# The loop over groups of a graph layer kernel, issued in source order instead of a scheduler's order

## The chip, the cores and the metric

The kernel runs on one core of a Trainium2 chip. The metric is the device time of one execution in microseconds. The core has four engines that compute: TensorE (PE in the profile; its weight loads are listed apart as PEld), VectorE (DVE), ScalarE (ACT) and GpSimd (POOL). SyncE (SP) issues the DMAs. TensorE writes its results to PSUM, from where VectorE and ScalarE read them.

## The reference, cut to what matters

There are 128 graphs of 128 nodes with 64 features. Layer 0 sums, for each node j, a ReLU over the neighbours that the mask of the adjacency matrix names. Layer 1 is a message pass with a gated update. Both end in a residual and a layer norm.

```python
# layer 0, per graph b
mask = (adj > 0.0)
h  = relu(x @ W1a [:, :, None] + (x_j - x_k) @ W1b + b1)     # for all pairs j, k
hm = einsum('bjkh,bjk->bjh', h, mask)                        # 192 wide
x  = layernorm(x + hm @ W2 + deg * b2)
# layer 1, per graph b
m   = relu(relu(x @ W1 + b1) @ W2 + b2)
msg = relu(adj @ m)
r, z, n = gates(msg @ W_ih.T + b_ih, x @ W_hh.T + b_hh)
x   = layernorm(x + (1 - z) * n + z * x)
```

The first layer is rewritten as u_j + v_k for each pair with an edge, so a ReLU sum becomes a sum of absolute values over the neighbours. The neighbours of each node are put into slots by 0/1 selection matrices.

## The kernel before, in words

The 128 graphs ("samples") are handled in 32 groups of G = 4. A group's work has three parts.

**Preparation** (`prep_steps`, 18 steps): masks (L303, POOL), ranks (L308 on PE, L310 on DVE), degrees, counts (eight small POOL operations, L321 to L336), offsets, turned, rows (L360, L369 on DVE), owners, places (L382 to L391), the selection matrices `pick0` and `pick1` (L398, 21 DVE operations), and `values(i)` for each sample. A `values` step is a chain: PE multiplies into `pu` (L409), ACT writes the first bf16 piece `b0` (L410) and `u` (L411), DVE takes the rest `r` (L413), ACT writes the second piece `b1` (L414), POOL writes the third (L415).

**Slots**: 16 stretches per group. Stretch (i, k) belongs to sample i and part k = 0 to 3; it is written "step 23" for i = 2, k = 3. In each, ACT first fills three PSUM banks (`pv`) with u, which is called the seed (L440). PE then adds 18 matrix products (9 where k is 2; L468). DVE then reduces the three banks by absolute value (L474). There are two such `pv` buffers, so the seed of a stretch has to wait until the reduce of the stretch two before has read the buffer. After k = 0, `before` runs (PE L448, ACT L450 and L452, DVE L453); after k = 2 POOL adds parts (L482, L483); after k = 1 `sums` of the sample before run (PE L494 to L497, ACT L498).

**Tail** (`tail_steps`, 11 steps): the second matrix product (L189) and residual (L191), a layer norm (DVE statistics L166 and L168, then four POOL operations L170 to L175), a transpose (L202), three message steps (L207 to L221), two gate steps (L230 to L236), the update (ACT L242, POOL L244 to L250), and the second layer norm with the store.

The main loop over groups writes these parts in one mixed order. While the slots of group g are written, the tail of group g-1 and the preparation of group g+1 are written between them as "side" steps, two after each stretch. In the source, the seed of the next stretch stands before the slots of the present one, and the side steps stand after them:

```python
ahead = seed(next stretch)
slots(s, i, k, p)
if k == 1 and pend:
    sums(*pend)
...
side[n]()
```

For a group in the middle of the run the loop's arithmetic puts the side steps thus:

| step | side steps | step | side steps |
|---|---|---|---|
| 00 | none | 20 | message3, turned |
| 01 | load, masks | 21 | gates (first half), values(2) |
| 02 | residual0, ranks | 22 | gates (second half), rows |
| 03 | second (L189), values(0) | 23 | update, places |
| 10 | norm0, degrees | 30 | norm1, picks (5) |
| 11 | turn (L202), counts | 31 | owners, picks (5) |
| 12 | message1, values(1) | 32 | values(3), picks (5) |
| 13 | message2, offsets | 33 | pick1 (3 + 3) |

The kernel is written in a tile framework. [...] Each engine runs its queue in the order in which it stands. [...] Tiles with the tag `w` (the small PSUM results of all side steps) share two buffers, so a PE operation of a side step waits until the `w` tile two before it has been read.

## Time and profile before

| what | value |
|---|---|
| median of 10 runs | 1481.21 us (1478.55 to 1488.22) |
| the profiled execution's own time | 1478.4 us |
| its span | 1476.6 us, clock granted 0.982 |
| PE busy | 1292.0 us, 87% |
| PEld busy | 1142.3 us, 77% |
| DVE busy | 1042.7 us, 71% |
| ACT busy | 916.2 us, 62% |
| POOL busy | 755.7 us, 51% |
| DMA | 23.36 MB, mean 16 GB/s |

The profile shows one execution, and the busy times sum the instructions of each engine. The rank product `pc` (L308) runs once for each group: its first run is at 13.4 us, its second at 31.2 us and its last at 1361.9 us. The busy shares in 40 slices are alike from the third slice to the next to last, so the run is one long regular stretch with a short start and end.

### The profile page before, as it was taken

How to read it: one execution, taken by the hardware profiler on the slowest of the kernel's cores; microseconds unless marked ns; L12 is line 12 of the kernel's file. 1: busy time of each engine (PE TensorE's matmuls, PEld its weight loads, DVE VectorE, ACT ScalarE, POOL GpSimd, SP SyncE). 2: the span in 40 equal slices, each digit the busy share in tenths (PEclk: the TensorE clock that was granted, in tenths of full speed). 3: DMA queues.
4: the chain of work that ended last, by engine and by line, in shares of the span. 5: the costliest groups of instructions: out<-in, count | busy, mean ns of one | idle time of the engine just before them, and what ended most of it. 6: DMA issues, size and time to landing. Idle time of an engine off the chain costs nothing.

```text
span 1476.6 us, 32123 instructions
## 1 busy us (share of the span) xinstructions
PE 1292.0 (87%) x12810; PEld 1142.3 (77%) x12810; DVE 1042.7 (71%) x2265; ACT 916.2 (62%) x1666; POOL 755.7 (51%) x1134
## 2 busy tenths in 40 slices
PE   5889888989889889889899889898889898888894
PEld 3878778778778778778788778787778787777783
DVE  5877777777777777776777776777776777776761
ACT  4666666666666666666666666666666666656651
POOL 4454564554554455554555554455554555554532
PEclk9999999999999999999999999999999999999995
DMA  2000000000000000000000000000000000000000
GB/s 58 8 12 19 19 12 16 19 12 19 19 12 15 20 12 19 19 12 16 19 12 20 18 14 16 19 12 19 13 18 16 19 12 19 10 10 12 5 2 9
DMA packets 17604, 23.36 MB, mean 16 GB/s; under 512 B 2855, under 2 KB 11306, under 8 KB 17450
## 3 DMA queue, kind: packets, MB, share of 16 engines
q1 hardware_dynamic: 17450, 21.27, 4.9%
q8 instruction: 102, 1.67, 0.5%
q14 instruction: 52, 0.43, 0.1%
HBM read 17.06 MB, written 4.19 MB: 14 GB/s over the span
## 4 chain that ended last, share of the span: by engine, by line
PE 46%; DVE 27%; ACT 13%; POOL 11%; issue 3%; DMA 0%; SPq 0%; ACTq 0%; DVEq 0%; POOLq 0%
PE pv L468 22%; DVE part L474 16%; ACT pv L440 10%; DVE pick L398 5%; PE pw L189 4%; POOL maskT L303 3%; PE pu L409 3%; DVE stats L166 2%; PE pm L207 2%; PE pa L220 2%; PE ph L494 2%; PE pn L213 2%; PE pg L232 2%; POOL ub L246 2%; PE ph L495 2%
## 5 line engine op out<-in xcount | busy, mean ns | idle before, releaser
L468 PE MATMUL pv<-b,pick 128*128 128x192 bf16 x8064 | 764.2, 248 | 118.2 <-ACT pv L440 115.1
L468 PEld LDWEIGHTS <-pick 128*128 128x128 bf16 x8064 | 682.8, 99 | 187.2 <-issue 165.4
L474 DVE TENSOR_REDUCE part<-pv 128x192 f32<-128x1152 f32 (+1 forms) x512 | 611.6, 1200 | 98.3 <-PE pv L468 92.8
L440 ACT COPY pv<-u 128x1152 f32<-128x1152 f32 (+1 forms) x384 | 370.0, 964 | 135.2 <-DVE part L474 135.0
L482 POOL TENSOR_TENSOR part<-part 128x384 f32<-128x384 f32 x128 | 127.6, 997 | 275.0 <-DVE part L474 275.0
L440 ACT COPY pv<-us 128x1152 f32<-128x1152 f32 x128 | 143.7, 1123 | 104.3 <-DVE part L474 104.2
L415 POOL TENSOR_TENSOR b<-r,b 128x384 bf16<-128x384 f32 x128 | 117.5, 918 | 98.3 <-ACT b L414 98.3
L413 DVE TENSOR_TENSOR r<-pu,b 128x384 f32<-128x384 f32 x128 | 70.7, 553 | 100.0 <-ACT u L411 100.0
L498 ACT COPY hmT<-ph 96x256 f32<-96x256 f32 x128 | 47.0, 368 | 133.2 <-PE ph L497 133.1
L398 DVE TENSOR_SCALAR pick<-rankT 128x512 bf16<-128x512 bf16 x480 | 126.1, 311 | 0.0
L410 ACT CAST b<-pu 128x384 bf16<-128x384 f32 x128 | 60.1, 470 | 86.5 <-PE pu L409 86.3
L409 PE MATMUL pu<-wuv,xT 65*128 65x384 f32 x256 | 110.9, 515 | 0.8 <-ACT deg L317 0.8
L303 POOL TENSOR_SCALAR maskT<-adjT 128x512 bf16<-128x512 f32 x32 | 50.2, 1569 | 111.2 <-PE ph L497 103.1
L494 PE MATMUL ph<-ident,part 128*96 128x128 f32 x512 | 102.4, 282 | 4.0 <-POOL part L483 4.0
L495 PE MATMUL ph<-ownT,part 128*96 128x128 f32 x512 | 98.4, 274 | 0.0
L235 DVE TENSOR_TENSOR rh<-rz,pg 128x128 f32<-128x128 f32 x64 | 18.4, 287 | 100.9 <-ACT rz L233 100.9
L189 PEld LDWEIGHTS pw<-w2c,hmT 96*128 96x128 f32 x512 | 63.7, 196 | 32.7 <-issue 30.7
L166 DVE BATCH_NORM_STATS2 stats<-y 128x6 f32<-128x64 f32 x256 | 38.6, 213 | 71.3 <-POOL y L250 71.2
L497 PE MATMUL ph<-maskT,b 128*96 128x128 bf16 x768 | 85.4, 220 | 0.0
L483 POOL TENSOR_TENSOR part<-part 128x192 f32<-128x192 f32 x128 | 75.9, 593 | 10.0
L414 ACT CAST b<-r 128x384 bf16<-128x384 f32 x128 | 65.5, 512 | 21.5 <-DVE r L413 21.2
L497 PEld LDWEIGHTS <-b 128*96 128x96 bf16 x768 | 73.5, 124 | 0.0
(122 smaller groups left out, 1810.3 us busy)
## 6 DMA issues: line engine op xcount, KB each, us to landing
adjT<-in_adjT_dram SPq DMA_DIRECT2D x32, 256.0 KB, 2.7
xT<-in_xT_dram SPq DMA_DIRECT2D x32, 128.0 KB, 3.4
x<-in_x_dram SPq DMA_DIRECT2D x32, 128.0 KB, 2.1
out_dram<-o SPq DMA_DIRECT2D x32, 128.0 KB, 1.7
bias<-piece SPq DMA_DIRECT2D x6, 0.5 KB, 2.2
wb<-in_w_dram SPq DMA_DIRECT2D x1, 48.0 KB, 2.2
wa<-in_w_dram SPq DMA_DIRECT2D x1, 48.0 KB
w2c<-in_w_dram SPq DMA_DIRECT2D x2, 24.0 KB, 1.8
```

The lines of the kernel that those rows point to most:

```text
L189: nc.tensor.matmul(p[:, i, :], s["hmT"][:, i, c, :], w2c[:, c, :], start=c == 0, stop=c == 1)
L303: nc.gpsimd.tensor_scalar(s["maskT"], s["adjT"], 0.0, None, ALU.is_gt)
L398: nc.vector.tensor_scalar(s[name][:, i], s[src], float(first + i), None, ALU.is_equal)
L409: nc.tensor.matmul(p, s["xT"][:, i, :], wuv, start=True, stop=True)
L415: nc.gpsimd.tensor_tensor(s["b2"][:, i, :], r, s["b1"][:, i, :], ALU.subtract)
L440: nc.scalar.copy(v, src.rearrange("p (c b h) -> p c b h", c=1, b=1).to_broadcast(list(v.shape)))
L468: nc.tensor.matmul(v[:, q[0], q[1], :], pick[:, j, i, :], s[f"b{c}"][:, i, H : 2 * H], start=False, stop=c == 2, skip_group_check=True,)
L474: nc.vector.tensor_reduce(s["part1"] if t else s["part"][:, k, :], v.rearrange("p c b h -> p h c b"), AX.XY, ALU.add, apply_absolute_value ...
L482: nc.gpsimd.tensor_tensor(f[:, 0:2], f[:, 0:2], f[:, 2:4], ALU.add)
L494: nc.tensor.matmul(p[:, c, :], part[:, 0, cs], ident, start=True, stop=False)
L495: nc.tensor.matmul(p[:, c, :], part1[:, cs], s["ownT"][:, i, :], start=False, stop=False)
L497: nc.tensor.matmul(p[:, c, :], s[f"b{b}"][:, i, vs], s["maskT"][:, i, :], start=False, stop=b == 2)
```

## The change

The loop over groups, with the first loads and the preparation of group 0 ahead of it and the last tail behind it, is put under a `with tc.manual_schedule():` block. In it every engine is given its instructions in the order of the source. No operation, tile, pool or size is changed; the rest of the diff is indentation.

```diff
-        load(states[0])
-        if ng > 1:
-            load(states[1])
-        for st in prep_steps(states[0]):
-            st()
...
+        with tc.manual_schedule():
+            load(states[0])
+            if ng > 1:
+                load(states[1])
+            for st in prep_steps(states[0]):
+                st()
...
+            for g in range(ng):
...
+                for i in range(G):
+                    for k in range(len(stretches)):
+                        p = ahead
+                        at += 1
+                        ahead = seed(states[todo[at][0]], todo[at][1], todo[at][2]) if at < len(todo) and k + 1 else None
+                        slots(s, i, k, p)
+                        if k == 1 and pend:
+                            sums(*pend)
+                            pend = None
...
+                            side[n]()
+                            n += 1
...
+            sums(*pend)
+            for st in tail_steps(states[ng - 1], work, ps_w, G, storer(ng - 1)):
+                st()
```

Built, the two kernels hold the same instructions. In a group from the middle of the run TensorE's queue is nearly the same in both. VectorE's and ScalarE's differ: the kernel before spreads the `pick` operations singly and in pairs between the reduces and has the statistics of the first layer norm directly behind L191; the changed kernel has the picks in blocks of five and six in steps 30 to 33, and those statistics behind step 10's L453. Before, ScalarE writes `b1` (L414) after the next seed in three of the four `values` steps, and `most` (L452) late; in the changed kernel the order is always `b0`, `u`, `b1`, then the next seed.

More of the change, by code (lines that the diff above doesn't have):

```diff
@@ L503, in storer @@
             return lambda o: nc.sync.dma_start(out[:, g * G : (g + 1) * G, :], o)
-        load(states[0])
-        if ng > 1:
-            load(states[1])
-        for st in prep_steps(states[0]):
-            st()
-        todo = [(g, i, k) for g in range(ng) for i in range(G) for k in range(len(stretches))]
-        ahead = seed(states[0], 0, 0)
-        pend = None
-        at = 0
-        per = G * len(stretches)
-        for g in range(ng):
-            s = states[g]
-            first, second = [], []
-            if g > 0:
-                first = tail_steps(states[g - 1], work, ps_w, G, storer(g - 1))
-            if g + 2 < ng:
-                second.append(lambda g=g: load(states[g + 2]))
-            if g + 1 < ng:
-                second += prep_steps(states[g + 1])
-            side = [second.pop(0)] if second else []
-            while first or second:
-                if len(second) * (per + 1) >= len(first) * (per + 1) and second:
-                    side.append(second.pop(0))
-                if first:
-                    side.append(first.pop(0))
-            n = 0
-            for i in range(G):
-                for k in range(len(stretches)):
-                    p = ahead
-                    at += 1
-                    ahead = seed(states[todo[at][0]], todo[at][1], todo[at][2]) if at < len(todo) and k + 1 else None
-                    slots(s, i, k, p)
-                    if k == 1 and pend:
-                        sums(*pend)
-                        pend = None
-                    if k == len(stretches) - 1:
-                        pend = (s, i, s["part"], s["part1"])
-                    if i == 0 and k == 0:
-                        continue
-                    while n < len(side) and (n + 1) * (per - 1) <= (i * len(stretches) + k) * (len(side) + 1):
-                        side[n]()
-                        n += 1
-            for st in side[n:]:
-                st()
-            if g > 0:
-                states[g - 1].clear()
@@ L552, in adj_resnorm_kernel @@
-        sums(*pend)
-        for st in tail_steps(states[ng - 1], work, ps_w, G, storer(ng - 1)):
-            st()
+        with tc.manual_schedule():
[3 more added lines that the diff above has]
+            for st in prep_steps(states[0]):
+                st()
+            todo = [(g, i, k) for g in range(ng) for i in range(G) for k in range(len(stretches))]
+            ahead = seed(states[0], 0, 0)
+            pend = None
+            at = 0
+            per = G * len(stretches)
+            for g in range(ng):
+                s = states[g]
+                first, second = [], []
+                if g > 0:
+                    first = tail_steps(states[g - 1], work, ps_w, G, storer(g - 1))
+                if g + 2 < ng:
+                    second.append(lambda g=g: load(states[g + 2]))
+                if g + 1 < ng:
+                    second += prep_steps(states[g + 1])
+                side = [second.pop(0)] if second else []
+                while first or second:
+                    if len(second) * (per + 1) >= len(first) * (per + 1) and second:
+                        side.append(second.pop(0))
+                    if first:
+                        side.append(first.pop(0))
+                n = 0
+                for i in range(G):
[6 more added lines that the diff above has]
+                            sums(*pend)
+                            pend = None
+                        if k == len(stretches) - 1:
+                            pend = (s, i, s["part"], s["part1"])
+                        if i == 0 and k == 0:
+                            continue
+                        while n < len(side) and (n + 1) * (per - 1) <= (i * len(stretches) + k) * (len(side) + 1):
+                            side[n]()
+                            n += 1
+                for st in side[n:]:
+                    st()
+                if g > 0:
+                    states[g - 1].clear()
+            sums(*pend)
+            for st in tail_steps(states[ng - 1], work, ps_w, G, storer(ng - 1)):
+                st()
```

## The prediction

> **What bounds the kernel now.** I read first the busy shares and the chain that ended last:

> ```profile
> PE 1292.0 (87%) x12810; PEld 1142.3 (77%) x12810; DVE 1042.7 (71%) x2265; ACT 916.2 (62%) x1666; POOL 755.7 (51%) x1134
> ...
> PE 46%; DVE 27%; ACT 13%; POOL 11%; issue 3%; DMA 0%; SPq 0%; ACTq 0%; DVEq 0%; POOLq 0%
> ```

> PE is the busiest, but more than half of the chain lies on other engines: PE waits for them now and then. DMA is no part of it. Next, one group from the middle (694.42 to 738.61 us, from the k = 2 slots of step 02 to those of the next group), by its busy times and by who waited:

> ```profile
> 694.42:738.61 44.19, 39.58 (x403) 35.20 (x402) 32.25 (x70) 28.51 (x52) 23.45 (x35) 1.00 0.06 16
> ```
> ```profile
> PE pv L468 <- ACT pv L440: 3.7, 4, 2.5
> PE pc L308 <- POOL maskT L303: 0.9, 1, 0.9
> ```

> Columns of the first: length, then busy time of PE, PEld, DVE, ACT, POOL. PE is busy for 39.58 us and idle for 4.6, nearly all of it waiting for a seed. The rank product `pc` comes each 44.36 us on average ((1361.9 - 31.2) / 30), so this group stands for the run. The largest wait is one of 2.51 us, here from the timeline (start, length, engine):

> ```profile
> 729.27 0.60 DVE L166 BATCH_NORM_STATS2 stats<-y 128x6 f32<-128x64 f32 x4 [2.23 <-POOL y L250]
> ...
> 729.79 0.36 DVE L168 BATCH_NORM_AGGREGATE mv<-stats 128x2 f32<-128x6 f32 x4
> ...
> 730.07 1.32 DVE L474 TENSOR_REDUCE part<-pv 128x192 f32<-128x1152 f32 x1
> ...
> 731.48 1.12 ACT L440 COPY pv<-us 128x1152 f32<-128x1152 f32 x1 [2.33 <-DVE part L474]
> ...
> 732.66 0.57 PE L468 MATMUL pv<-b,pick 128*128 128x192 bf16 x5 [2.51 <-ACT pv L440]
> ```

> The scheduler put the second norm's statistics ahead of a reduce; POOL was late with `y`; DVE held the reduce behind it, so the seed and then PE were late. That is what a badly placed instruction costs in a queue. The `values` chain is the other place to look:

> ```profile
> 700.54 0.48 ACT L410 CAST b<-pu 128x384 bf16<-128x384 f32 x1 [2.45 <-PE pu L409]
> 700.92 0.33 ACT L411 COPY u<-pu 128x192 f32<-128x192 f32 x1
> 701.48 1.12 ACT L440 COPY pv<-u 128x1152 f32<-128x1152 f32 x1 [0.24 <-DVE part L474]
> 702.54 0.51 ACT L414 CAST b<-r 128x384 bf16<-128x384 f32 x1
> 702.95 0.31 ACT L450 COPY us<-pz 128x192 f32<-128x192 f32 x1
> ```

> The seed goes ahead of `b1` (L414). In source order it goes behind.

> **Durations.** An instruction's follower on the same engine starts about 0.1 us before its record ends: ACT's 0.48 cast is followed after 0.38, its 1.12 seed after 1.06. So I use the start-to-start distance for what merely queues, and the whole record for what depends. Distances from the timeline: slots 1.48 (0.74 for k = 2; results 0.17 later), sums 1.24, `pu` 0.67, second (L189) 1.73, `pz` 0.25, `pd` 0.16, `pt` 0.44, `pm` 0.95, `pn` 0.87, `po` 0.10, `pa` 1.00, `pr` 0.24, a gate half 1.08, places 0.66, `pq` 0.22, `pc` 0.21; together 38.1 us of PE per group. ACT: b0 0.37 (record 0.47), u 0.21 (0.32), b1 0.42, us 0.21, most 0.36 (0.46), seed 1.12. DVE: reduce 1.26 (1.35), r 0.47 (0.56), L453 0.33, statistics 0.80, five picks 1.0, each `side` 0.69, own 0.45. A hand-over costs 0.03 to 0.08.

> **What is removed.** In the changed order the second norm's statistics stand in step 30 behind its reduce and L453. Tanh starts after step 30's seed, POOL's four operations take 3.3 us (row 725.96 to 729.27), and `y` is there 1.4 us before DVE comes to it. The wait of 2.51 goes. Two waits on a seed of some 0.3 to 0.6 each go or are replaced by those below.

> **What is added**, walking a middle group step by step (distance on the late chain, minus the PE work beside it):

> 1. Step 03, values(0). From the end of `pu` to the next slots but one: 0.20 + b0 0.37 + u 0.32 + 0.05 + r 0.56 + 0.03 + b1 0.42 + seed 1.12 + 0.06 = 3.13. PE has slots 1.48, pz 0.25 and pd 0.16. Wait **1.24**.
> 2. Step 11, `turn`. The first norm's statistics now stand behind L453, which needs `most`, which stands behind that late seed. From the start of step 11's slots: seed began 1.18 before; + 1.05 + 0.21 + 0.46 + 0.05 = L453 at 0.59, + 0.33, statistics 0.88, then POOL ve, rs, yc, x 2.9 (rows 699.89 to 702.78) and hand-overs 0.14: x1 at 4.84. PE has 1.48 + 1.24. `pt` waits **2.13**, and the slots queue behind it.
> 3. Step 12, values(1): 3.13 against slots 1.48, pn 0.87, po 0.10: **0.68**. (`pm` waits 0.09 for its copy.)
> 4. Step 21, values(2): 3.13 against slots 0.74 and gates 1.08: **1.31**.
> 5. Step 22, rows: DVE does rh, n, both sides and own before reduce 23, and `places` needs own: from the slots of step 23, own at 2.65 + 0.05 + the last eight products 0.44 = 3.14, against 2.14: **1.00**; the late reduce then costs the next seed **0.26**.
> 6. Step 30: reduce, L453, statistics and five picks stand before reduce 31: 1.70 + 1.26 + 0.33 + 0.80 + 1.00 + 1.35 + 0.05 + 1.12 + 0.06 = 7.67 from the slots of step 30 to those of step 33; PE has 6.34: **1.33**.
> 7. Step 32, values(3), where b0 also waits for the seed of step 33: 2.93 from there, PE has 1.61: **1.32**. Then 0.13 for the seed of 01.
> 8. maskT (L303) behind `sums`, as now: **0.9**.

> Sum 10.4 us of PE waits. By the same count (the waits named by the profile plus the 0.17 in which the last product drains, five times) the group of before has 4.6 + 0.85 = 5.45. The difference is 4.95 us per group. Over 30 periods that is 148.5 us.

> **Start and end.** In the changed order all of group 0's preparation stands before its first seed; by the same distances (at the slow early clock of rows 13.77 to 29.28) the slots of step 03 start near 37 instead of 35.06 us: +2. Groups 0 and 31 have half of the side steps; bounds 0 to +10, I take +2 for both. The last tail, 35 us of one thin chain, keeps its order: 0. DMA: SP's load of a group waits until `message3` of step 20 frees the adjacency tile and is used in step 01 of the next group, some 28 us later at 49 us a group; a 256 KB load lands in 2.7 us, so it is covered, and the store in step 30 holds nothing back.

> Sum: 1478.4 + 148.5 + 4 = **1631 us** for the profiled execution (1476.6 span plus 1.8 around it); it lies 0.2% below the median of 1481.21, which is inside the spread.

> [...] The trace has POOL's L175 at 861 ns in the first norm, where picks run beside it, and at 612 in the second, where a reduce from PSUM does. [...]

> **Rivals.**

> - *Milder* (0.14). The waits in items 2 and 6 rest on several queues in a row; if a late PE lets the others catch up there and half of both is hidden, 1.7 us of 4.95 go: 1478 + 30 x 3.2 + 4 = 1578; with all of item 2 hidden too, 1550. For it: DVE is busy for only 32 of 44 us.
> - *Harsher* (0.13). If followers wait for whole records and not for the distances, my walk gives a period of 52.1 against 44.2: 30 x 7.9 + 4, that is 1719. Against it: rows that overlap by 0.1 throughout the trace.
> - *Faster* (0.06). The mechanism is the wait of 2.51 at step 30 that goes, with 0.75 at step 13 (slots of step 12 issued by 706.57, those of 13 from 707.32); if nothing replaces them, 30 x 3.26 less: 1381. It decides when the 3.13 us of the `values` chain finds that much PE work beside it; the rows above give 1.8 to 2.5.
> - *No change* (0.03). TensorE's queue hardly differs between the two built programs, and PE is the busiest engine; the waits might only change places: 1478 within 5. Against it: PE's order is not what makes it wait. That the region might not take effect is excluded by the built order of the other queues.

> **How the numbers follow.** The forecast (0.64) holds for 3.9 to 6.2 us per group: 1597 to 1670 with its edges. A run of this kernel can tell about 0.3% from no change. Slower: 0.64 + 0.14 + 0.13 = 0.91; same 0.03; faster 0.06. The range reaches into the milder and the harsher case: 1550 to 1705.

> **What the next profile should show.** PE idle per middle group near 9 us, by waits of `pv` on ACT, of `pt` (L202) on POOL x (L175), now 13.4 us in all, near 2 us per group, and of `ps` on DVE own; the period of `pc` near 49.3 us; POOL `y` no longer named before L166; ACT's seed directly behind `b1`. If `pt` does not wait, item 2 is wrong; if the period is under 46, the cover I counted as missing was there; if ACT or POOL show longer records, contention has entered that the trace of before does not hold.

## The result, and the profile after

The changed kernel takes 1703.17 us (median of 9 runs, 1696.48 to 1710.86) against 1481.38 for the kernel before (31 runs): 1.1484 times as long, 95% interval 1.1457 to 1.1512. It is slower, as forecast, and by more: 222 us where 152 were expected. The time lies just inside the range of 1550 to 1705, at its upper end, and outside the edges of the forecast proper, 1597 to 1670.

From the page of the changed kernel: its span, the busy shares, and the chain that ended last by engine.

```profile
span 1699.4 us, 31903 instructions
...
PE 1312.4 (77%) x12810; PEld 1148.1 (68%) x12810; DVE 1114.1 (66%) x2265; ACT 922.9 (54%) x1666; POOL 789.3 (46%) x1134
...
PE 37%; DVE 24%; POOL 19%; ACT 16%; issue 3%; DMA 0%; SPq 0%; ACTq 0%; DVEq 0%; POOLq 0%
```

Every engine has as many instructions as before; PE's busy time rose by 20 us only. POOL's share of the chain rose from 11 to 19%, though POOL is the least busy engine: others now wait for it. DVE and POOL are busy for 71 and 34 us longer with the same number of instructions, so some of their records are longer.

A middle group of the changed kernel, by its busy times (period, PE, PEld, DVE, ACT, POOL, then PE's clock):

```profile
699.36:750.65 51.29, 40.17 (x401) 35.37 (x400) 34.55 (x70) 28.73 (x53) 25.01 (x36) 1.00 0.04 14
```

And who kept PE waiting in it (us in total, times, longest):

```profile
PE pv L468 <- ACT pv L440: 7.2, 7, 1.8
PE pt L202 <- POOL x L175: 1.7, 1, 1.7
PE pc L308 <- POOL maskT L303: 0.9, 1, 0.9
PE ps L386 <- DVE side L360: 0.7, 1, 0.7
PE ps L389 <- DVE own L369: 0.6, 1, 0.6
```

The clock is full; PE simply waits 11.1 us where it waited 4.6. The transpose waits for x1, places for own, and seven stretches instead of four wait for a late seed. These are the waits that the forecast listed. One was listed at 0.13 only: the 1.78 at the head of the first line, ahead of the slots of step 01. The changed kernel's VectorE with the three blocks of five picks (steps 30, 31 and 32), and then its GpSimd in the same place:

```profile
735.88 1.07 DVE L398 TENSOR_SCALAR pick<-rankT 128x512 bf16<-128x512 bf16 x5
...
738.13 1.09 DVE L398 TENSOR_SCALAR pick<-rankT 128x512 bf16<-128x512 bf16 x5
739.13 0.75 DVE L474 TENSOR_REDUCE part<-pv 128x192 f32<-128x576 f32 x1
740.09 0.56 DVE L413 TENSOR_TENSOR r<-pu,b 128x384 f32<-128x384 f32 x1 [0.20 <-ACT u L411]
740.56 2.85 DVE L398 TENSOR_SCALAR pick<-rankT 128x512 bf16<-128x512 bf16 x5
743.33 1.34 DVE L474 TENSOR_REDUCE part<-pv 128x192 f32<-128x1152 f32 x1
```

```profile
736.05 0.98 POOL L170 TENSOR_SCALAR ve<-mv 128x4 f32<-128x4 f32 x1 [2.59 <-DVE mv L168]
...
738.12 1.57 POOL L174 TENSOR_TENSOR yc<-y,mv 128x256 f32<-128x256 f32 x1
739.77 0.61 POOL L175 TENSOR_TENSOR o<-yc,rs 128x256 f32<-128x256 f32 x1
740.34 1.00 POOL L482 TENSOR_TENSOR part<-part 128x384 f32<-128x384 f32 x1
741.42 0.72 POOL L483 TENSOR_TENSOR part<-part 128x192 f32<-128x192 f32 x1
742.10 0.96 POOL L415 TENSOR_TENSOR b<-r,b 128x384 bf16<-128x384 f32 x1
```

The block of step 32 takes 2.85 us, the other two 1.07 and 1.09. All three have GpSimd work beside them, so that alone does not set the price. In steps 30 and 31 the GpSimd operation began as the picks did or just behind them, and it was GpSimd that grew: L170 to 0.98 and L174 to 1.57, where their medians are 0.23 and 0.62. In step 32 GpSimd was already at work with three operations in a row, and the picks grew (shortest, median and longest of the five in ns):

```profile
L398 DVE TENSOR_SCALAR pick<-rankT x5: 280/675/997, 740.6 to 743.1; 128x512 bf16<-128x512 bf16 x5
```

Three of these five started while L482, L483 or L415 ran, and each ended some 0.15 us behind it; the other two took 0.28. Reduce 33 stands behind the block, so it starts 2 us late.

The kernel before has a block of five too. It ran beside short GpSimd operations and was not lengthened; L327 was (0.53 where it takes 0.23 in the changed kernel):

```profile
706.55 1.09 DVE L398 TENSOR_SCALAR pick<-rankT 128x512 bf16<-128x512 bf16 x5
...
706.95 0.53 POOL L327 TENSOR_SCALAR nseg_all<-rnd 128x4 bf16<-128x4 f32 x1
```

**Where the 223 us of the span came from.** `pc` (L308) marks the groups. From its second to its last run the kernel before takes 1330.6 us and the changed one 1532.9: 202.2, or 6.74 per period. The start is 12.2 us longer (43.4 against 31.2 at the second `pc`), the end 8.4 (123.1 after the last `pc`, against 114.7).

### The profile page after: what moved, and what is told of

It is laid out like the page before. It is cut to its first block, busy times and chain, and to the rows that moved or that the text cites. A ratio compares the mean times of both kernels' runs of the same rounds, so it can differ in the third digit from the quotient of the medians.

```text
span 1699.4 us, 31903 instructions
## 1 busy us (share of the span) xinstructions
PE 1312.4 (77%) x12810; PEld 1148.1 (68%) x12810; DVE 1114.1 (66%) x2265; ACT 922.9 (54%) x1666; POOL 789.3 (46%) x1134
## 4 chain that ended last, share of the span: by engine, by line
PE 37%; DVE 24%; POOL 19%; ACT 16%; issue 3%; DMA 0%; SPq 0%; ACTq 0%; DVEq 0%; POOLq 0%
PE pv L468 15%; DVE part L474 8%; DVE pick L398 8%; ACT pv L440 7%; PE pu L409 4%; DVE r L413 4%; PE pw L189 3%; ACT b L410 3%; POOL maskT L303 3%; ACT b L414 3%; POOL ua L244 2%; POOL rs L172 2%; PE pa L220 2%; DVE stats L166 2%; PE pm L207 2%
## 5 line engine op out<-in xcount | busy, mean ns | idle before, releaser
L468 PE MATMUL pv<-b,pick 128*128 128x192 bf16 x8064 | 755.9, 247 | 227.7 <-ACT pv L440 227.7
L468 PEld LDWEIGHTS <-pick 128*128 128x128 bf16 x8064 | 680.5, 98 | 345.1 <-issue 322.1
L474 DVE TENSOR_REDUCE part<-pv 128x192 f32<-128x1152 f32 (+1 forms) x512 | 615.2, 1202 | 305.7 <-PE pv L468 273.4
L440 ACT COPY pv<-u 128x1152 f32<-128x1152 f32 (+1 forms) x384 | 369.8, 963 | 133.1 <-DVE part L474 129.0
L415 POOL TENSOR_TENSOR b<-r,b 128x384 bf16<-128x384 f32 x128 | 118.6, 927 | 449.9 <-ACT b L414 446.0
L398 DVE TENSOR_SCALAR pick<-rankT 128x512 bf16<-128x512 bf16 x480 | 164.7, 409 | 0.0
L440 ACT COPY pv<-us 128x1152 f32<-128x1152 f32 x128 | 143.3, 1119 | 24.3 <-DVE part L474 24.2
L482 POOL TENSOR_TENSOR part<-part 128x384 f32<-128x384 f32 x128 | 128.3, 1002 | 55.6 <-DVE part L474 52.9
L303 POOL TENSOR_SCALAR maskT<-adjT 128x512 bf16<-128x512 f32 x32 | 48.2, 1507 | 181.9 <-PE ph L497 174.4
L410 ACT CAST b<-pu 128x384 bf16<-128x384 f32 x128 | 61.1, 477 | 129.0 <-PE pu L409 128.9
L409 PE MATMUL pu<-wuv,xT 65*128 65x384 f32 x256 | 113.2, 525 | 1.6 <-DVE r L413 1.3
L414 ACT CAST b<-r 128x384 bf16<-128x384 f32 x128 | 65.5, 512 | 87.2 <-DVE r L413 87.2
L170 POOL TENSOR_SCALAR ve<-mv 128x4 f32<-128x4 f32 x64 | 32.7, 511 | 146.6 <-DVE mv L168 146.6
L483 POOL TENSOR_TENSOR part<-part 128x192 f32<-128x192 f32 x128 | 91.8, 717 | 10.0
L495 PEld LDWEIGHTS ph<-ownT,part 128*96 128x96 f32 x512 | 70.0, 164 | 0.3 <-DVE part L474 0.3
```

The source lines that it names most:

```text
L398: nc.vector.tensor_scalar(s[name][:, i], s[src], float(first + i), None, ALU.is_equal)
L409: nc.tensor.matmul(p, s["xT"][:, i, :], wuv, start=True, stop=True)
L410: nc.scalar.copy(s["b0"][:, i, :], p)
L414: nc.scalar.copy(s["b1"][:, i, :], r)
L415: nc.gpsimd.tensor_tensor(s["b2"][:, i, :], r, s["b1"][:, i, :], ALU.subtract)
L440: nc.scalar.copy(v, src.rearrange("p (c b h) -> p c b h", c=1, b=1).to_broadcast(list(v.shape)))
```

## The experiments

All edits are made to the changed kernel. Line numbers move with an edit (the picks are L419 in e7, e8 and e9 and L417 in e5), so lines are named by what they write. Differences are taken between medians, with the changed kernel at 1703. The kernel before, run again beside them, took 1479 to 1484 us, so a difference of a few microseconds means nothing here.

**e1: `b1` behind the next seed.** The rest of a `values` step is kept in a list and written after the next seed.

```diff
-                    nc.scalar.copy(s["b1"][:, i, :], r)
-                    nc.gpsimd.tensor_tensor(s["b2"][:, i, :], r, s["b1"][:, i, :], ALU.subtract)
+                    def rest():
+                        nc.scalar.copy(s["b1"][:, i, :], r)
+                        nc.gpsimd.tensor_tensor(s["b2"][:, i, :], r, s["b1"][:, i, :], ALU.subtract)
+                    late.append(rest)
...
                         ahead = seed(...)
+                        while late:
+                            late.pop(0)()
```

> Changed kernel, with b1 (L414) and the POOL piece b2 of each values step written behind the next seed, not ahead of it. Queue theory: the three waits of PE on a late seed that lie behind a values chain and nothing else (1.13, 0.56 and 1.19 us per group in the trace) go; the fourth (1.14) only moves to the next step, since the seed of step 01 is bound by VectorE's picks; the wait of the transpose on x1 grows by 0.7 because its chain hangs on L453. Net 2.2 us of 51.1 per group: near 1637 us (1620 to 1655). Rival, contention between VectorE's picks and GpSimd sets the period: under 0.5 us per group, over 1688 us.

Measured: 1755.26 us, ratio 1.1816 (1.1733 to 1.1899). Slower than the changed kernel by 52 us. The time falls under the rival's "over 1688", but neither theory had a loss. PE's waits of a group with a nearly full clock (1536.32 to 1587.33, 51.01 us long):

```profile
PE pv L473 <- ACT pv L445: 4.3, 3, 2.9
PE pt L202 <- POOL x L175: 2.3, 1, 2.3
PE ps L388 <- DVE side L362: 1.5, 1, 1.5
PE pc L310 <- POOL maskT L305: 0.9, 1, 0.9
PE ps L391 <- DVE own L371: 0.5, 1, 0.5
```

The waits behind the `values` chains did go: 7 waits on a seed became 3. But what they saved PE lost again further on, at places that were bound by another chain: x1 from 1.7 to 2.3, own from 1.3 to 2.0, step 01 from 1.78 to 2.9. Only 1.6 us of waits were saved, and the remaining ones were longer. That brought in the clock. Two-microsecond pieces of another group of e1 (length, busy times, then the granted clock):

```profile
685.00:687.00 2.00, 0.55 (x6) 0.54 (x7) 0.00 (x0) 0.00 (x0) 1.74 (x5) 1.00 0.00 0
687.00:689.00 2.00, 2.00 (x11) 1.15 (x10) 0.63 (x1) 1.60 (x2) 1.31 (x6) 0.55 0.00 0
689.00:691.00 2.00, 2.00 (x4) 0.61 (x3) 0.13 (x1) 0.68 (x1) 1.58 (x2) 0.50 0.00 0
691.00:693.00 2.00, 2.00 (x12) 1.43 (x11) 0.50 (x1) 1.23 (x3) 0.00 (x0) 0.50 0.00 0
693.00:695.00 2.00, 2.00 (x19) 1.95 (x17) 0.63 (x2) 0.93 (x2) 0.91 (x1) 0.74 0.00 0
```

PE idles for 2.27 us ahead of the transpose and then runs at half its clock for some 7 us. The group of these pieces (675.15 to 729.25) takes 54.10 us at a mean clock of 0.91, the one above 51.01 at 0.97. The mean over all 30 periods is 53.2. By these groups the loss of e1 is the clock's, and its small gain is what a removed wait is worth while the next chain is as late. In both groups 2.27 us of idle time ahead of the transpose were enough: in the one above, the nine products behind it took 1.65 us where they take 0.91. The last section shows what else it depends on.

**e2: the first norm directly behind L191.**

```diff
             s["y0"] = y
+            norm0()
...
-        return [residual0, second, norm0, turn, ...
+        return [residual0, second, none, turn, ...
```

> Changed kernel, with the whole first layer norm written directly behind L191 in step 03, ahead of values(0), instead of in step 10. Queue theory: x1 is ready some 2 us before PE comes to the transpose; the wait of 1.70 plus 0.17 of drain goes and nothing takes its place: 1.9 us per group, near 1646 us (1635 to 1665). Rival, the waits change places because another queue is as late (the seed of step 13, or r behind the statistics): under 0.6 us per group, over 1685 us.

Measured: 1637.15 us, ratio 1.1054 (1.1021 to 1.1087); 66 us less, 59 of them in the 30 periods between the second and the last `pc`. The wait of the transpose is gone from a middle group and the other lines stand as they were:

```profile
PE pv L472 <- ACT pv L444: 7.2, 7, 1.8
PE pc L312 <- POOL maskT L307: 0.9, 1, 0.9
PE ps L390 <- DVE side L364: 0.7, 1, 0.7
PE ps L393 <- DVE own L373: 0.6, 1, 0.6
```

**e4: GpSimd's additions of the fourth sample a step later.**

```diff
-            if k == 2:
+            if k == (3 if i == G - 1 else 2):
                 f = s["part"]
```

> Changed kernel, with GpSimd's two additions L482 and L483 of each group's fourth sample written in step 33, behind b2, instead of step 32. Contention theory: the third block of five picks, which took 2.85 us beside L482, L483 and L415, comes down towards the 1.07 of the other blocks; the wait of the slots of step 01 falls from 1.78 to 0.3 to 0.8: 1.0 to 1.5 us per group, 1658 to 1673 us. Rival, the block is long for a reason in VectorE's own queue (r ahead of it, the operands): no change, 1698 to 1708 us.

Measured: 1676.56 us, ratio 1.1303 (1.1261 to 1.1346); 27 us less, a little short of the 30 to 45 expected. The block of picks comes down from 2.85 to 1.80, with L415 in its old place, and the wait ahead of step 01 falls from 1.78 to 0.73:

```profile
782.11 1.80 DVE L398 TENSOR_SCALAR pick<-rankT 128x512 bf16<-128x512 bf16 x5
```

The order of VectorE's instructions is the same, so the block was long because of what GpSimd did beside it.

**e6: rows in step 20.** The call of `rows` stands at the end of `turned`, and its own place is empty.

> Changed kernel, with the rows step (L360, L369) written in step 20 behind turned instead of in step 22. Queue theory: places finds own ready, its waits of 0.70 and 0.65 go, reduce 23 starts some 2.5 us earlier and with it the 0.19 of the seed after it: 1.5 us per group, near 1656 us (1645 to 1670). Rival, the two sides delay reduce 21 and the seed of step 23 instead: under 0.5 us per group, over 1688 us.

Measured: 1649.15 us, ratio 1.1139 (1.1105 to 1.1172); 54 us less, and no wait of `ps` in a middle group.

**e5: the picks of pick0 spread.** They are written in twos and threes in steps 11, 12, 13, 23, 31 and 32; all else in the loop keeps its place. In group 0's preparation, ahead of the loop, `owners` and `values(3)` also come ahead of the picks.

> Changed kernel, with only the fifteen picks of pick0 spread: two or three in each of steps 11, 12, 13, 23, 31 and 32 in place of five in each of 30, 31 and 32. Queue theory: reduce 31 no longer stands behind a block, so the 1.16 before the slots of step 33 falls to some 0.3, and reduce 33 no longer stands behind the 2.85 us block, so the 1.78 before step 01 falls to some 1.0: 1.6 us per group, near 1655 us (1640 to 1675). Rival, the two-buffer ring of seed, slots and reduce sets these waits whatever stands between: under 0.5 us per group, over 1688 us.

Measured: 1643.28 us, ratio 1.1085 (1.1022 to 1.1148); 60 us less. The waits on a seed fall from 7.2 to 5.3 us per group. The second `pc` is 4.7 us earlier (38.7 against 43.4), and the 30 periods from there are 51 us shorter, so the blocks cost a little less than the first norm.

**Three moves together (e2, e4, e6).**

> Changed kernel, with the first norm behind L191, the late GpSimd additions and the early rows together; b1 stays ahead of the seed. Separate waits: the gains of the three (66, 27 and 54 us) add, near 1556 us (1540 to 1580). Rival, the waits hide one another: the gains add to less than two thirds, over 1605 us.

Measured: 1557.50 us, ratio 1.0493 (1.0442 to 1.0544); 146 us less, where the single gains add to 147. The waits were separate.

**The three moves and `b1` behind the seed.**

> The three moves and b1 with b2 behind the next seed. Queue theory with a clock that falls after long idle stretches: with x1, own and the seed of step 01 early there is no idle stretch of PE over 2 us, the clock stays near 0.98, and the three seed waits of 1.13, 0.56 and 1.19 us go: 1470 to 1515 us. Rival, b1 behind the seed lowers the clock or delays the chain wherever it stands: no gain over the three moves, 1550 us or more, with a granted clock under 0.95.

Measured: 1482.55 us, ratio 0.9992 (0.9970 to 1.0013): the kernel before's time again. The edit that cost 52 us alone now saves 75, 2.5 per group where the three waits made 2.88. The clock was 0.963 in the mean; groups at 0.96 take 44.5 to 44.8 us, those at 1.00 take 43.7 to 44.3. So the clock did not stay up as was expected: a wait of 1.80 us is left ahead of the slots of step 33 (1.09 with three moves), and behind it the clock fell in 17 of 29 groups from the middle. The four moves take back 221 of the 222 us, but they do not restore the order of before (the picks are still in blocks, the wait of 2.51 is still gone), so that the two times are equal is in part chance.

**e7: an order planned from the trace.** Side steps get named places in a table, with the same operations. `b1` stands behind the next seed and `rows` and the first norm are early, as in e1, e2 and e6; GpSimd's additions keep their old place:

```python
PLAN = [  # steps 00, 01, 02, 03, 10, ...
    "", "load masks", "residual0", "ranks second norm0 values0",
    "degrees", "turn counts p0a", "message1 values1 p0b", "message2 offsets p0c",
    "message3 turned rows", "gates0", "gates1 p0d", "update places",
    "", "norm1 p0e p1a", "values3 p0f p1b", "values2 owners p1c"]
```

> Manual region with the side steps at places chosen from the trace: the four ideas above, picks in twos and threes, ranks behind the slots of step 03, values(2) and owners in step 33, the second norm behind reduce 31. Same operations. Queue theory: PE's work of 38.1 us plus some 0.6 of drains and 1.5 of waits, a period near 40.5 us and 1380 us (1350 to 1430). Rival, the scheduler's order of the kernel before is as good as the two-buffer ring allows: 1470 us or more.

Measured: 1476.19 us, ratio 0.9948 (0.9923 to 0.9973). It is half a per cent faster than the kernel before, but 96 us over what was expected; the number is the rival's. In step 32 five picks again met GpSimd's additions and took some 2.6 us ahead of reduce 33; the slots of step 01 waited 2.17, and with that the clock dropped in four groups of five (44.7 us; 43.07 with the full clock). e8 shows that the rival's reason, that the two-buffer ring allows no better, was not the cause.

**e8: the plan mended.**

```diff
-    "", "load masks", "residual0", "ranks second norm0 values0",
-    "degrees", "turn counts p0a", ...
+    "", "load masks", "residual0 values0", "ranks second norm0",
+    "degrees p0a", "turn counts p0b", "message1 values1 p0c", "message2 offsets p0d",
+    "message3 turned rows", "gates0", "gates1 p0e", "update places p0f",
+    "owners p1a", "norm1 p1b", "values3", "values2 p1c"]
```

> The planned order with the faults seen in its trace mended: no picks in step 32 (they met GpSimd's additions there and took 2.6 us in front of reduce 33, which cost the 2.17 before step 01), values(0) in step 02 so that PE has work while the seed of step 03 is made (0.73), owners in step 30 (0.51). Queue theory: no idle stretch of PE over 1 us, clock near 1.00 in every group, period 40.0 to 41.0, near 1355 us (1335 to 1395). Rival, contention of picks and GpSimd moves with the picks and takes the gain back: 1420 us or more.

Measured: 1375.57 us, ratio 0.9275 (0.9242 to 0.9308): 7% faster than the kernel before, with the same instructions, in the range expected and 20 us above its middle value. A middle group of e8, first its times, then all of PE's waits in it:

```profile
652.44:693.45 41.01, 39.21 (x403) 35.17 (x401) 34.78 (x70) 28.51 (x53) 22.98 (x36) 1.00 0.06 17
```

```profile
PE pv L500 <- ACT pv L472: 1.7, 4, 0.7
```

PE is busy for 39.2 of 41.0 us, and the clock is full. No wait of PE is over 0.7. e8 changes several places at once, and no run tells them apart.

**e9: e8 with the second norm early again,** written at the end of step 23.

> The kernel e8 with one thing moved: the second norm (norm1) written at the end of step 23, so that its statistics stand ahead of reduce 30 as in the kernel before. Queue theory: VectorE waits there for GpSimd's y, reduce 30 and the seed of step 32 come later, PE idles 1.0 to 2.5 us more per group, 30 to 80 us more than e8 (more where the clock falls). Rival, a wait of VectorE at that place is covered by the second buffer: within 10 us of e8.

Measured: 1405.75 us, ratio 0.9481 (0.9444 to 0.9518): 30 us more than e8, the low end of what was expected. VectorE waits for POOL's `y` for 48.0 us in all (3.0 in e8). A group takes 41.5 us with the full clock, 0.5 more; in about one group of four the clock drops and it takes 43.0. So the misplaced step costs here too, but less than the 2.51 for which PE waited behind it in the kernel before.

## Why the prediction was right in its direction and short in its size

- **PE waits for seeds in the kernel before; the order of the other queues sets them: right.** In the changed kernel, e1, e2, e4, e6 and the runs with three and four moves PE's 12810 instructions run in exactly the same order, and the times reach from 1483 to 1755 us.
- **What is removed (2.51 per group): right.** L166 waits for POOL y for 5.4 us in all after, 71.2 before. (The profile now puts 0.96 us ahead of reduce 30 down to `y`, which ends at 733.47; but the slots that reduce 30 reads end at 733.35, so at most 0.1 of it is lost.) e9 shows that such a place costs in another order as well; the price there was not 2.5.
- **Items 1, 3, 4 (the `values` chain, 1.24, 0.68, 1.31): right in the order and nearly in size.** Measured 1.13, 0.56 and 1.19, to which the drain of 0.17 that my count contains has to be added. That they are worth their time was shown by the four moves against three. e1 showed that this holds only while nothing else is as late.
- **Item 2 (the transpose, 2.13): right.** Measured 1.70 and 0.17; e2 gave 66 us, 59 of them in the 30 periods, 1.97 each. x1's L175 takes 613 ns (median) here, where nothing runs on VectorE beside it, instead of a median of 861 before, where picks did. These 0.25 us are nearly all by which the count was too high: its 2.9 for POOL was taken from the rows of before.
- **Item 5 (rows, 1.00 and 0.26): right place, too small.** Measured 0.70 + 0.65 and 0.19. `own` came 3.37 us after the slots of step 23 began, not 2.65: VectorE's sides ran beside POOL's ua (1.17 us where it took 0.72) and own itself took 0.83 instead of 0.45. e6 gave 54 us.
- **Items 6 and 7 (1.33, 1.32): right**, 1.16 and 1.14 with 0.17 each.
- **"Then 0.13 for the seed of 01": this is the step that failed.** Measured 1.78. I took a block of five picks at 1.0 us and did not ask what GpSimd would be doing when it came to its new place. The 1.0 is what the block at 706.55 us of the kernel before took (whose picks do not all stand singly or in pairs); beside it GpSimd was held up, not the picks. In step 32 the block met three GpSimd operations of 0.7 to 1.0 us, two of them the additions that e4 moves. e4 moved only GpSimd's work and brought the block from 2.85 to 1.80. The prediction had named longer POOL records as the sign of contention, and they came: L483 takes 717 ns in the mean, 593 before. I had L175 before me, at 861 ns beside picks and 612 without them, and did not ask what that would mean at the place where the picks arrive.
- **Start and end, +4: wrong, 20.6.** The first slots of the changed kernel start at 31.84 and take 3.04 us instead of 1.65, after 3.02 us of idle time, and the second `pc` is 12.2 us late. I had two for the start, from slots of step 03 near 37; they start at 44.24. The end lost 8.4; there the transpose and the seeds wait once more as in the middle. Both are read from the trace alone; no run tests them.
- **The sum.** By my count PE's waits are 12.8 us instead of 10.4 per group: 1.8 of the difference is step 01, 0.6 is item 5, and the rest cancels. A middle group grew by 7.1 (51.30 against 44.19) where 4.95 were expected; with group 0's shorter period the 30 periods came to 202 instead of 148.5, and the ends to 20.6 instead of 4.
- **The rivals.** The harsher case named 1719, near the result, but for another reason (whole records instead of distances). That the result still lies in the range is luck: the range was drawn up to 1705 for that case, and not for contention. The distances held, since items 1, 3 and 4 came out within 0.06 of the count once the drain is added, and item 2 below it. No wait changed places in the way of the case "no change"; in e1 waits did so, and there it mattered.

What stays open: the start and the end, which no run tests; what each change of place in e8 is worth; and whether the clock falls after a piece of time that is about half idle (last section).

## What to carry to other kernels

Source order is neither good nor bad: the same instructions took 1703 us in the order in which they stood, 1481 in the scheduler's and 1376 in one planned from the trace. For each instruction that gets a new place, ask what is queued behind it, and what the other engine is doing when it comes there: for picks on VectorE that was GpSimd, and one of the two took longer (a block of five picks 2.85 us instead of 1.07, or L174 1.57 instead of 0.62). Take the waits out together, and look at the clock: a removed wait that only makes the next one longer can cost more than it gave (52 us in e1).

## What the runs showed of the hardware that was not expected

Five bf16 picks on VectorE took 1.07 and 1.09 us while one GpSimd operation beside them was held up (L170 0.98 instead of 0.23, L174 1.57 instead of 0.62), 2.85 where GpSimd was already at work with the first of three operations, and 1.80 in e4, where of these only L415 kept its place. Of the 672 single picks in the trace of the changed kernel, 114 took over 0.35 us: each of them started while a GpSimd operation ran and ended 0.14 or 0.15 us behind it. None of the 341 that started while GpSimd had nothing running was so long. Which of the two engines is held up when both start close together, these rows do not settle: in the changed kernel L170 at 119.63 us began while a pick ran and grew to 0.98, while L415 at 30.84 us began so too, took 0.95, and the next pick took 1.00.

```profile
328.25:331.66 3.41, 1.60 (x14) 1.10 (x12) 2.68 (x11) 1.07 (x3) 2.40 (x4) 1.00 0.00 0
331.66:335.08 3.42, 2.71 (x18) 2.50 (x18) 0.99 (x2) 3.32 (x7) 2.83 (x5) 0.50 0.26 77
...
727.60:731.02 3.42, 2.55 (x26) 2.04 (x25) 1.75 (x9) 0.85 (x2) 2.26 (x6) 1.00 0.00 0
731.02:734.43 3.41, 1.77 (x20) 1.62 (x20) 2.01 (x5) 2.95 (x5) 3.18 (x5) 1.00 0.11 38
734.43:737.84 3.41, 3.41 (x40) 3.30 (x39) 2.95 (x3) 2.35 (x5) 0.91 (x1) 1.00 0.14 38
```

The first wait leaves one piece idle for 1.81 us, and the clock is halved in the next piece; the second is split into 0.87 and 1.64, and the clock stays. Counted over the middle of all twelve traces, from 45 us after the start to 125 us before the end, with the clock full: each of the 61 pieces with more than 2.02 us idle was followed by a halved clock, none of the 4447 with less than 1.55, and 47 of the 256 between. In the traces of the two kernels alone the same counts are 1 of 1, none of 763 and 5 of 56. So in these traces a wait lowers the clock where it takes up about half of one such piece or more, and in between the idle time alone does not tell.
